# Six attention blocks ahead of the FFN instead of nine, ordered by a clock model, in a gated cross-attention and top-1 expert kernel

## The chip, the cores and the metric

The kernel runs on one core of a Trainium2 chip. The metric is the device time in microseconds (us) of one execution, as the median of several runs. A core has five engines that run side by side, each with its own queue of instructions: PE (TensorE, matrix products; its weight loads are shown as PEld), DVE (VectorE), ACT (ScalarE), POOL (GpSimd) and SP (SyncE, used here to issue transfers). ACT also issues some transfers from its queue. An engine takes its instructions strictly in the order in which the program lists them, and waits where one needs another engine's or a transfer's result.

## What is computed

For 4 batches of 2048 rows with 512 columns, all in float32:

```python
def _L0_xattn_ref(query, ref, Wq, bq, Wk, bk, Wv, bv):
    Q = query @ Wq + bq
    K = ref @ Wk + bk
    V = ref @ Wv + bv
    scores = jnp.einsum('bqh,bkh->bqk', Q, K)
    attn = jax.nn.softmax(scores, axis=-1) * norm_fact
    return jnp.einsum('bqk,bkh->bqh', attn, V)

def _L0_ffn_ref(x, Wr, br, W1, b1, W2, b2):
    scores = jnp.einsum('bh,he->be', x.mean(axis=1), Wr) + br
    top1 = jnp.argmax(scores, axis=-1)
    ...
    h = jax.nn.relu(jnp.einsum('bnh,bhf->bnf', x, w1) + c1[:, None, :])
    return jnp.einsum('bnf,bfh->bnh', h, w2) + c2[:, None, :]

x = x + jnp.tanh(g_xattn[0]) * _L0_xattn_ref(_layernorm(x), ctx_1024, ...)
x = x + jnp.tanh(g_ffn[0]) * _L0_ffn_ref(_layernorm(x), ...)
```

The context has 128 rows for each batch. There are 8 experts with W1 of 512 x 2048 and W2 of 2048 x 512; each batch uses one, chosen by the mean of its normalised rows, so the expert of a batch is known only when all of that batch's attention is done.

## The kernel before

**Attention** is cut into 16 blocks (4 batches of NBLK = 4 blocks of TB = 512 rows). The keys and the query matrix are folded into one matrix M for each batch (`keys`, L339; `values`, L370 makes V). A block (`attention`, L168) loads x (L179) and its transpose xT (L182); takes the row statistics on DVE (st, L189) with the inverse deviation rstd on POOL (L195); forms the scores psc = xT·M on PE (L204), which DVE scales into sc (L211); takes the maximum on DVE (nmax, L219) and the exponential on ACT (L222); transposes it on PE (pp, L231) with a copy pT by ACT (L234); multiplies by V on PE (pav, L245), with DVE adding the result into x (L249); takes statistics again; stores the new x to DRAM (x1d, L259); normalises it to z on ACT (L263), in place of x; transposes z on PE (pt, L278), with ACT copying to zT (L282) and adding up the columns (zsum); and stores zT to DRAM (z2d, L288). zT has a tile of its own in the pool of xT.

**The FFN** runs in 16 stages (batch, one of NF = 2 halves of its rows, one of two halves fh of the 2048 features). Each stage is `ffn1` (L748) and `ffn2` (L869). Both use a two-level scheme with 7 products in place of 8 at each level, so sums of weights and sums of z are needed as operands. X, Y and Q are the PSUM banks into which the products go (L631); ACT copies X to Y (L650) between products, and DVE, ACT and POOL build the results from them. The sums of z are made by `z_prepare` (L682: L706 outer on POOL or DVE, L702 inner on POOL) from z2d.

**Weights.** `stage_w1` (L536) and `stage_w2` (L553) load an expert's weights as `base` (L478, L487), make the sums on POOL (`outer_sums`, L445, four subtractions; `inner_sums` calls it on the inner level) and store the results to DRAM tensors W1d and W2d (L466). `fetch` (L590) brings the operands back into a ring of NW = 5 tiles w (L616), issued by SP in the order of their use. `route` (L398) finds the expert (pr, L409; ei, L423), reads the number into SP's register (L426) and loads b1T.

**Order around the change.** The program is written out by Python generators, and their interleaving is each engine's order; no scheduler changes it. Ahead of the FFN, EARLY = 9 blocks run as `streams`, each starting `skew` = 13 steps after the one before, and inside a block the tuple `lag` (AT_ONCE or, in the FFN, LATER) says how many steps to let pass at certain places. Every third step one piece of `others` (keys and values of batches 1 to 3) is put in. The end of batch 0's fourth block starts `first_expert` (L948): route, then `stage_first` (L493) on POOL, which sums the first half of W1 in four pieces; a store is issued AGE steps after its sum (`later`, `settle`). In the FFN, `tick` (L1028) is called between products and lets the remaining seven blocks (`slow`) and the staging of weights (`staged`) advance by counters with the rates PACE. Loads of x go by SP ahead of the FFN and by ACT in it.

Of the kernel before, what the change touches and what calls it, by code (L numbers as in the profile page):

```python
# [11 lines left out]
F32 = mybir.dt.float32  # L12
# [6 lines left out]
P = 128  # L19
# [70 lines left out]
def flamingo(tc, ctx, x, xT, cxT, g_x, g_f, WqT, Wk, Wv, bqk, bv, Wr, br, W1, b1, W2, b2, out):  # L90
# [43 lines left out]
    nc.vector.tensor_scalar(gx, gx, float(1.0 / np.sqrt(H).astype(np.float32)), None, ALU.mult)  # L134
    iota_e = const.tile([P, E], F32, name="iota_e")
# [8 lines left out]
    for b in range(B):  # L144
# [7 lines left out]
        for fh in range(2):  # L152
            for lo, n in ((0, 4), (4, 3)) if b + fh else ((0, 2), (2, 2), (4, 3)):
                t = dram.tile([P, n, 2, 7, P], F32, name=f"W1d_{b}{fh}{lo}")
                W1d.update({(b, fh, lo + i): (t, i) for i in range(n)})
            W2d[b, fh] = dram.tile([P, 2, 4, 2, Q], F32, name=f"W2d_{b}{fh}")

    zsum = {}
    MV = {}

# [5 lines left out]


    def attention(b, blk, pools):  # L168


        xp, xTp, wk, ps_t, ps_a, queue, lag = pools

        def wait(n):
            for _ in range(n):
                yield

        Mb, Vb = MV[b]
        xt = xp.tile([P, 4, H], F32, tag="x", name=f"x_{b}_{blk}")
        queue.dma_start(xt, rows(x, b, blk))  # L179
        yield from wait(lag[5])  # L180
        xTt = xTp.tile([P, KC, TB], F32, tag="xT", name=f"xT_{b}_{blk}")
        nc.sync.dma_start(xTt, xT[b, blk].rearrange("p c t q -> p c (t q)"))  # L182
        yield from wait(lag[6])

        def statistics():
            mv = small.tile([P, 4, 2], F32, tag="mv", name="mv", bufs=4)
            for t in range(4):
                st = small.tile([P, 6], F32, tag="st", name="st", bufs=4)
                nc.vector.bn_stats(st, xt[:, t, :])  # L189
                nc.vector.bn_aggr(mv[:, t, :], st)  # L190
                yield
# [4 lines left out]
            yield  # L196
            return mv, rstd

        _, rstd = yield from statistics()
        psc = ps_a.tile([P, 4, S], F32, tag="pa", name="psc")  # L200
        sc = wk.tile([P, 4, S], F32, tag="wk", name="sc")
        for t in range(4):
# [5 lines left out]
            if t % 2:  # L208
                yield
        for t in range(4):  # L210
# [4 lines left out]
            if t % 2:  # L215
                yield
# [3 lines left out]
        yield  # L220
        for t in range(4):
# [4 lines left out]
            if t % 2:  # L226
                yield
        yield from wait(lag[0])
# [3 lines left out]
        yield  # L232
        pT = wk.tile([P, TB], F32, tag="wk", name="pT")
        nc.scalar.copy(pT, pp)  # L234
        coef = small.tile([P, 4], F32, tag="coef", name="coef", bufs=4)
        nc.vector.reciprocal(coef, ssum)
        nc.vector.tensor_scalar(coef, coef, gx, None, ALU.mult)
        yield
        yield from wait(lag[1])
        pav = {}  # L240
        for t in range(5):
            if t < 4:
                ps, tag = ((ps_a, "pa"), (ps_t, "pt"))[t % 2]
                pav[t] = ps.tile([P, H], F32, tag=tag, name="pav")
                nc.tensor.matmul(  # L245
                    pav[t], lhsT=pT[:, t * P : (t + 1) * P], rhs=Vb, start=True, stop=True
                )
            if t:
                nc.vector.scalar_tensor_tensor(  # L249
                    xt[:, t - 1, :], pav[t - 1], coef[:, t - 1 : t], xt[:, t - 1, :],  # L250
                    ALU.mult, ALU.add,
                )
            yield
        mv, rstd = yield from statistics()
        yield from wait(lag[2])
        shift = small.tile([P, 4], F32, tag="shift", name="shift", bufs=4)
        nc.vector.scalar_tensor_tensor(shift, mv[:, :, 0], -1.0, rstd, ALU.mult, ALU.mult)
        yield
        queue.dma_start(x1d[b, blk], xt)  # L259
        yield from wait(lag[3])  # L260
        z = xt
        for t in range(4):
# [4 lines left out]
            yield  # L267
        yield from wait(lag[4])
        if blk == 0:
            zsum[b] = small.tile([P, KC, NBLK], F32, tag="zsum", name=f"zsum_{b}", bufs=2)  # L270
        zT = xTp.tile([P, KC, TB], F32, tag="xT", name=f"zT_{b}_{blk}")
        pt = {}
        for kc in range(KC + 1):
            if kc < KC:
                ps, tag = ((ps_t, "pt"), (ps_a, "pa"))[kc % 2]
                pt[kc] = ps.tile([P, TB], F32, tag=tag, name="pt")
                for t in range(4):
                    nc.tensor.transpose(  # L278
                        pt[kc][:, t * P : (t + 1) * P], z[:, t, kc * P : (kc + 1) * P], ident
                    )  # L280
            if kc:
                nc.scalar.activation(  # L282
                    zT[:, kc - 1, :], pt[kc - 1], AF.Copy,
                    accum_out=zsum[b][:, kc - 1, blk : blk + 1],
                )
            yield
        yield from wait(lag[7])
        queue.dma_start(z2d[b, blk], zT)  # L288
        yield
# [3 lines left out]
    xp, xTp, wkp = pool("xp", 1), pool("xTp", 1), pool("wk", 2)  # L293
    ps_t, ps_a = pool("ps_t", 1, space=PSUM), pool("ps_a", 1, space=PSUM)
    first, setup = ExitStack(), ExitStack()


    AT_ONCE, LATER = (4, 2, 3, 7, 4, 3, 8, 3), (2, 1, 3, 6, 3, 3, 8, 0)

    EARLY = 9  # L300
    three = (
        pool("x0", 5, first), pool("xT0", 3, first), pool("wk0", 4, first),
        pool("ps_t0", 2, first, space=PSUM), pool("ps_a0", 2, first, space=PSUM), nc.sync, AT_ONCE,
    )
    mv1 = pool("mv1", 1, first)
    one = (xp, xTp, wkp, ps_t, ps_a, nc.sync, AT_ONCE)
    ps_k = pool("ps_k", 2, first, space=PSUM)
    sp = pool("setup", 1, setup, side="right")
    if True:
        M0 = sp.tile([P, KC, S], F32, name="M0")  # L310
        V0 = sp.tile([P, H], F32, name="V0")
        MV[0] = (M0, V0)
        ctxT0 = sp.tile([P, 1, KC, S], F32, name="ctxT0")
        ctxTr = sp.tile([P, B - 1, KC, S], F32, name="ctxTr")
        w = {name: sp.tile([P, KC, H], F32, name=f"w{name}") for name in ("k", "q", "v")}
        nc.sync.dma_start(ctxT0, cxT[:, 0:1])
        for c in range(2):
            nc.sync.dma_start(w["k"][:, :, c * Q : (c + 1) * Q], Wk[:, :, c * Q : (c + 1) * Q])
        nc.sync.dma_start(w["q"], WqT)
        bvb = sp.tile([P, H], F32, name="bvb")  # L320
        with nc.allow_non_contiguous_dma(reason="bias"):
            nc.scalar.dma_start(bvb, bv.partition_broadcast(P))
        bqb = sp.tile([P, KC, P], F32, name="bqb")
        nc.vector.tensor_copy(bqb, bqk_t[:, 0:KC].unsqueeze(2).to_broadcast([P, KC, P]))
        order = [(b, blk) for b in range(B) for blk in range(NBLK)][:EARLY]
        streams = [attention(*i, one if i == order[-1] else three) for i in order]
# [3 lines left out]
        for m in range(KC):  # L330
            st = small.tile([P, 6], F32, tag="st", name="st", bufs=4)
            mq = small.tile([P, 2], F32, tag="mq", name="mq", bufs=2)
            nc.vector.bn_stats(st, w["q"][:, m, :])
            nc.vector.bn_aggr(mq, st)
            nc.vector.tensor_scalar(
                w["q"][:, m, :], w["q"][:, m, :], mq[:, 0:1], None, ALU.subtract
            )

        def keys(cT, n, KT, M, pc_out):  # L339

            for m in range(KC):
                pk = ps_k.tile([P, n, S], F32, tag="pk", name="pk")
                for kc in range(KC):
                    nc.tensor.matmul(  # L344
                        pk, lhsT=w["k"][:, kc, m * P : (m + 1) * P], rhs=cT[:, :, kc, :],
                        start=kc == 0, stop=kc == KC - 1,
                    )
# [4 lines left out]
                yield  # L352
            for kc in range(KC):
                pm = ps_k.tile([P, n, S], F32, tag="pk", name="pm")
                for m in range(KC):
                    nc.tensor.matmul(  # L356
                        pm, lhsT=w["q"][:, m, kc * P : (kc + 1) * P], rhs=KT[:, m, :],
                        start=m == 0, stop=m == KC - 1,
                    )
                nc.scalar.copy(M(kc), pm)  # L360
                yield
            pc = ps_k.tile([P, n * S], F32, tag="pk", name="pc")
            for m in range(KC):
                nc.tensor.matmul(
                    pc, lhsT=bqb[:, m, :], rhs=KT[:, m, :], start=m == 0, stop=m == KC - 1
                )
            nc.scalar.copy(pc_out, pc)
            yield

        def values(cT, V):  # L370
            pv = ps_k.tile([P, H], F32, tag="pk", name="pv")
            for kc in range(KC):
                nc.tensor.matmul(  # L373
                    pv, lhsT=cT[:, kc, :], rhs=w["v"][:, kc, :], start=kc == 0, stop=kc == KC - 1
                )
            nc.vector.tensor_tensor(V, pv, bvb, ALU.add)

# [342 lines left out]
    h = {}  # L720
# [374 lines left out]
```

## Time and profile before

| what | value |
|---|---|
| median of 3 runs | 1777.44 us (1776.56 to 1781.16) |
| profiled execution | 1777.29 us, of which the span of the core 1775.3 us |
| mean granted PE clock | 0.982 |
| busy: DVE, ACT, POOL | 1042.1, 581.2, 681.2 us |
| first FFN matmul | 193.76 us |
| z2d of the fourth block issued | 139.55 us |
| expert number ready; base load issued | 150.9; 153.06 us |

The span runs from the first to the last instruction of the profiled execution. Busy times are the sums of an engine's instructions; where an engine is not busy, it waits, and the profile names the instruction or transfer that ended the wait. The granted clock is the share of the full clock at which PE was allowed to run.

### The profile page before, as it was taken

The page shows a single profiled execution, that of the slowest core. Times are in us where ns is not written, and L with a number is a line of the kernel's source. Part 1 is how long each engine was busy: PE and PEld are TensorE (multiplying, and loading weights), DVE is VectorE, ACT ScalarE, POOL GpSimd, SP SyncE. Part 2 cuts the span into 40 slices and gives each one's busy share as a digit, 9 for nine tenths or more (in the row PEclk, how much of TensorE's full clock was granted, in tenths as well). Part 3 has the DMA queues.
Part 4 walks back from the last instruction along what each step waited for, and adds up shares of the span by engine and source line. Part 5 has one row for each costly group of instructions (what it writes and reads, how often), then busy time and mean ns, then how long its engine had stood idle before and what let it go on. Part 6 is the DMA issues. An engine that isn't in the chain of part 4 may idle for free.

```text
span 1775.3 us, 21897 instructions
## 1 busy us (share of the span) xinstructions
PE 1688.1 (95%) x7894; PEld 1432.4 (81%) x7894; DVE 1042.1 (59%) x1632; ACT 581.2 (33%) x1277; POOL 681.2 (38%) x564
## 2 busy tenths in 40 slices
PE   7977688999999899999999999999999999999998
PEld 5545477888878788888888888888888888888887
DVE  3678267584666647666564736474846463646362
ACT  1245531433415134251524323242424141415150
POOL 0128463476435454235532564056513410251010
PEclk9998899999999999999999999999999999999999
DMA  7487795786838678485856666565757452536241
GB/s 290 155 317 270 304 336 212 244 301 237 338 132 298 252 246 322 163 303 175 306 177 226 215 220 243 191 217 194 272 183 238 162 180 84 190 125 199 77 141 70
DMA packets 145562, 390.76 MB, mean 220 GB/s; under 512 B 10672, under 2 KB 40368, under 8 KB 130864
## 3 DMA queue, kind: packets, MB, share of 16 engines
q1 hardware_dynamic: 141568, 367.07, 58.6%
q10 hardware_dynamic: 3888, 22.31, 3.2%
q8 instruction: 63, 1.03, 0.2%
q14 instruction: 43, 0.35, 0.1%
HBM read 269.28 MB, written 120.06 MB: 219 GB/s over the span
## 4 chain that ended last, share of the span: by engine, by line
PE 86%; DVE 6%; DMA 4%; POOL 2%; issue 1%; ACT 0%; SPq 0%; DVEq 0%; POOLq 0%; ACTq 0%
PE Y L631 34%; PE Q L631 23%; PE X L631 22%; PE pav L245 2%; PE psc L204 2%; DVE st L189 1%; DMA w<-in_W_dram 1%; DVE h L726 1%; DVE y L894 1%; PE pt L278 1%; PE pk L344 1%; PE pm L356 1%; DMA W1d<-tt 1%; DVE x L249 1%; PE pv L373 1%; POOL tt L448 1%
## 5 line engine op out<-in xcount | busy, mean ns | idle before, releaser
L631 PE MATMUL Y<-z,w 128*128 128x256 f32 x1344 | 335.2, 383 | 15.1 <-DMA w<-W1d 5.8
L448 POOL TENSOR_TENSOR base<-base 128x512 f32<-128x512 f32 (+2 forms) x152 | 212.4, 1406 | 234.7 <-DMA base<-in_W_dram 207.1
L631 PEld LDWEIGHTS Y<-z,w 128*128 128x128 f32 x1344 | 252.2, 191 | 59.4 <-issue 9.8
L763 ACT ACTIVATE h<-c,b1T 128x256 f32<-128x256 f32 x512 | 229.9, 501 | 70.9 <-DVE c L791 29.6
L650 ACT COPY Y<-X 128x512 f32<-128x512 f32 x144 | 82.3, 571 | 469.4 <-PE X L631 469.2
L631 PE MATMUL X<-w,h 128*128 128x256 f32 x1024 | 230.0, 381 | 3.1 <-DMA w<-in_W_dram 3.0
L631 PE MATMUL Y<-w,h 128*128 128x256 f32 x1024 | 229.8, 382 | 0.0
L631 PE MATMUL Q<-w,h 128*128 128x256 f32 x1024 | 227.1, 379 | 0.0
L631 PEld LDWEIGHTS X<-w,h 128*128 128x128 f32 x1024 | 195.1, 191 | 34.2 <-issue 6.3
L631 PEld LDWEIGHTS Y<-w,h 128*128 128x128 f32 x1024 | 196.5, 192 | 30.7 <-issue 4.0
L631 PE MATMUL Q<-z,w 128*128 128x256 f32 x896 | 217.7, 383 | 0.6
L631 PE MATMUL X<-z,w 128*128 128x256 f32 x896 | 215.7, 380 | 1.6 <-DMA w<-W1d 1.6
L631 PEld LDWEIGHTS Q<-w,h 128*128 128x128 f32 x1024 | 194.2, 190 | 26.6 <-issue 0.5
L702 POOL TENSOR_TENSOR z<-z 128x256 f32<-128x256 f32 x224 | 185.9, 855 | 52.1 <-DMA z<-z2d 25.3
L631 PEld LDWEIGHTS Q<-z,w 128*128 128x128 f32 x896 | 171.0, 192 | 25.6 <-issue 1.2
L631 PEld LDWEIGHTS X<-z,w 128*128 128x128 f32 x896 | 170.0, 191 | 25.0 <-issue 2.0
L782 POOL TENSOR_TENSOR r<-r,cg 128x512 f32<-128x512 f32 x32 | 40.5, 1267 | 375.5 <-DVE cg L837 359.7
L195 POOL TENSOR_TENSOR rstd<-ve,mhalf 128x4 f32<-128x4 f32 x32 | 35.8, 1120 | 277.9 <-DVE ve L194 277.6
L631 PE MATMUL Y<-w,s 128*128 128x256 f32 x512 | 114.4, 379 | 0.0
L894 DVE SCALAR_TENSOR_TENSOR y<-Y,gf,y 128x512 f32<-128x512 f32 x64 | 47.9, 749 | 110.2 <-PE Y L631 109.2
L245 PE MATMUL pav<-V,pT 128*128 128x512 f32 x128 | 73.0, 681 | 37.9 <-DVE x L249 26.0
L631 PEld LDWEIGHTS Y<-w,s 128*128 128x128 f32 x512 | 96.7, 190 | 15.0 <-issue 2.4
(120 smaller groups left out, 1894.9 us busy)
## 6 DMA issues: line engine op xcount, KB each, us to landing
w<-W1d SPq DMA_DIRECT2D x112, 512.0 KB, 4.2
w<-W1d SPq DMA_DIRECT2D x112, 384.0 KB, 3.5
w<-W2d SPq DMA_DIRECT2D x64, 512.0 KB, 6.6
base<-in_W_dram SPq DMA_DIRECT2D x31, 1024.0 KB, 6.7
W1d<-base SPq DMA_DIRECT2D x14, 1792.0 KB, 10.9
w<-in_W_dram SPq DMA_DIRECT2D x48, 512.0 KB, 5.1
W1d<-tt SPq DMA_DIRECT2D x16, 1344.0 KB, 7.0
xT<-in_xT_dram SPq DMA_DIRECT2D x16, 1024.0 KB, 10.7
```

The lines of the kernel that those rows point to most:

```text
L189: nc.vector.bn_stats(st, xt[:, t, :])
L195: nc.gpsimd.tensor_tensor(rstd, ve, mhalf, ALU.pow)
L204: nc.tensor.matmul(psc[:, t, :], lhsT=xTt[:, kc, t * P : (t + 1) * P], rhs=Mb[:, kc, :], start=kc == 0, stop=kc == KC - 1,)
L245: nc.tensor.matmul(pav[t], lhsT=pT[:, t * P : (t + 1) * P], rhs=Vb, start=True, stop=True)
L249: nc.vector.scalar_tensor_tensor(xt[:, t - 1, :], pav[t - 1], coef[:, t - 1 : t], xt[:, t - 1, :], ALU.mult, ALU.add,)
L448: eng.tensor_tensor(o, l, r, ALU.subtract)
L631: nc.tensor.matmul(bank[:, c, :], lhsT=left(k, c), rhs=right(k, c), start=fresh and c == 0 and k == 0, stop=c == 1 and k == ks - 1, skip_g ...
L650: nc.scalar.copy(t["Y"], t["X"])
L702: nc.gpsimd.tensor_tensor(a[o], a[l], a[r], op)
L763: nc.scalar.activation(h[ij][:, v, 2 * m + c, :], src[:, c, :], AF.Relu, bias=b1T[:, f + c : f + c + 1],)
L782: eng.tensor_tensor(r[j], r[j], v, ALU.add)
L894: nc.vector.scalar_tensor_tensor(o, v, gf, o, ALU.mult, ALU.add)
```

## The change

1. EARLY is 6 instead of 9. The four blocks of batch 0 run at the same time; the fifth block follows the first, the sixth follows the fourth.
2. Each generator now yields which engine its piece uses and for how many us by an estimate in the source; a class `Stream` keeps a time for each stream, and the stream with the smallest time goes next. The counters `lag`, `skew`, `AGE`, `GAP` and `LOAD` are gone. `places` and `room` count the tiles of a pool that are in use, so that a stream asks before it takes one.
3. The keys are made for batch 0, batch 1, and batches 2 and 3 together, in three goes; M and V of batch 1 are copied by ACT (`second`) and not sent through DRAM.
4. The first half of W1 is summed as two streams (`first_half`: `part(0)` and `part(1)`); `minus` gives each subtraction to DVE or POOL, whichever the model has free earlier. Each result is stored as soon as it is there. The sums of z of the first FFN half are shared in the same way (`lefts_`).
5. z goes to the tile of xT, and zT to the tile of x, which has one buffer in the FFN. pT goes to sc's place.
6. In the FFN the two streams advance by the model's time and PACE.

The core of the diff:

```diff
-        yield from wait(lag[2])
         shift = small.tile([P, 4], F32, tag="shift", name="shift", bufs=4)
         nc.vector.scalar_tensor_tensor(shift, mv[:, :, 0], -1.0, rstd, ALU.mult, ALU.mult)
-        yield
+        yield (("DVE", 0.2),)
         queue.dma_start(x1d[b, blk], xt)
-        yield from wait(lag[3])
-        z = xt
+        z = xTt.rearrange("p c q -> p (c q)").rearrange("p (t h) -> p t h", t=4)
...
-        zT = xTp.tile([P, KC, TB], F32, tag="xT", name=f"zT_{b}_{blk}")
+        zT = xt.rearrange("p t h -> p (t h)").rearrange("p (c q) -> p c q", c=KC)
...
-    EARLY = 9
+    EARLY = 6
+    START, SLACK = (14.0, 1.0, 2.0, 3.0), 0.3
+    PRESS = 0.3
...
+    def second():
+        yield from until(lambda: 1 in ready_kv and all((0, i) in done_at for i in range(NBLK)))
+        Mb = mvp.tile([P, KC, S], F32, tag="M", name="M_1")
+        Vb = mvp.tile([P, H], F32, tag="V", name="V_1")
+        nc.scalar.copy(Mb, Ms[:, 0])
+        nc.scalar.copy(Vb, Vs[1])
+        MV[1] = [Mb, Vb]
+        yield (("ACT", 1.2),)
...
+    def minus(eng, o, l, r):
+        name = {nc.gpsimd: "POOL", nc.vector: "DVE"}.get(eng)
+        if name is None:
+            name = min(("DVE", "POOL"), key=lambda n: free[n])
+            eng = {"POOL": nc.gpsimd, "DVE": nc.vector}[name]
+        eng.tensor_tensor(o, l, r, ALU.subtract)
+        return ((name, 0.2 + 2.1e-3 * int(np.prod(o.shape[1:]))),)
...
-    def stage_first(eng, x0):
+    def first_half():
...
+        def outer(pc):
+            t4, t1, t2 = outs[pc]
+            b11, b21, b22, b12 = (blocks[pc][i // 2][:, i % 2] for i in range(4))
+            for i, took in enumerate(outer_sums(None, b11, b21, b22, b12, t4, t1, t2)):
+                yield took
+                if i == 1:
+                    for k in range(2):
+                        keep(5 + k, 1, pc, outs[pc][1 + k].unsqueeze(1))
+                if i == 2:
+                    keep(4, 1, pc, t4.unsqueeze(1))
+            keep(2, 2, pc, blocks[pc][1])
+        def part(pc):
+            yield (("DMA", 8),)
+            for i in range(2):
+                yield from inner_sums(None, blocks[pc][i])
+                if i == 0:
+                    keep(0, 2, pc, blocks[pc][0])
+            yield from outer(pc)
+            fetched[pc] = 1
...
+    class Stream:
+        def step(self):
+            if not ahead_of_ffn[0]:
+                self.at = max(self.at, clock["now"])
+            chains = next(self.gen, False)
...
+                    for engine, us in chain_:
+                        if not ahead_of_ffn[0]:
+                            t += us * BUSY[engine]
+                            if engine == "PE":
+                                clock["now"] += us
+                        elif engine in free:
+                            t = free[engine] = max(free[engine], t) + us
...
+    while True:
+        s_ = min(parts, key=lambda s: s.at)
...
+            if first_at is not None and clock["now"] >= first_at and fetched == [1, 1] and 1 in Zs[0, 0]["made"] and not any(
+                t in parts for t in threes
+            ):
+                break
+        if not s_.step():
+            parts.remove(s_)
...
-    PACE = {"slow": (0.6, 0.7, 0.7), "staged": (1.3, 0.7, 0.5, 0.5)}
+    PACE = {"slow": (1.0,.7,.7), "staged": (3.0,3.,3.,3.)}
...
+    def paced(name, stream, more):
+        due[name] = min(due[name] + more, 1.0 + more)
+        while stream and due[name] >= 1 and stream.at <= clock["now"] + SOON:
+            due[name] -= 1
+            if not stream.step():
+                stream = None
+        return stream
```

`keep` stores a result to W1d at once. The loop that writes the order ahead of the FFN ends when the first weights have been fetched, both parts of the first half are summed and the blocks of the three-buffer pools are written; what is left of the last block and of the first expert's staging goes into the FFN.

## The prediction

> **What bounds the kernel now.** I read the page first: the busy totals, the row of granted clock, the chain that ended last.
>
> ```profile
> PE 1688.1 (95%) x7894; PEld 1432.4 (81%) x7894; DVE 1042.1 (59%) x1632; ACT 581.2 (33%) x1277; POOL 681.2 (38%) x564
> ...
> PE   7977688999999899999999999999999999999998
> ...
> PE 86%; DVE 6%; DMA 4%; POOL 2%; issue 1%; ACT 0%; SPq 0%; DVEq 0%; POOLq 0%; ACTq 0%
> ```
>
> TensorE (PE) is the bound, with 86% of the chain; 1775.3 - 1688.1 = 87.2 us of its span are idle. The slices show where: the first seven, of 44.4 us each. So next I read the windows.
>
> ```profile
> 100.00:150.00 50.00, 36.55 (x195) 25.65 (x196) 40.21 (x102) 22.62 (x66) 26.50 (x27) 0.88 0.85 325
> 150.00:200.00 50.00, 29.10 (x132) 18.87 (x131) 26.79 (x62) 25.62 (x66) 39.58 (x40) 0.81 0.74 284
> 200.00:250.00 50.00, 41.45 (x183) 34.84 (x184) 21.24 (x37) 19.28 (x43) 19.39 (x16) 0.90 0.84 305
> ...
> 300.00:350.00 50.00, 48.66 (x220) 41.34 (x221) 24.08 (x39) 16.82 (x34) 15.47 (x13) 0.95 0.71 246
> ...
> 1000.00:1050.00 50.00, 50.00 (x233) 43.88 (x232) 24.73 (x27) 7.09 (x13) 38.59 (x37) 1.00 0.56 195
> ```
>
> After window and length come busy PE, PEld, DVE, ACT, POOL and the granted clock. An idle PE costs twice: 29.10 of 50 us busy in 150 to 200, and those at a clock of 0.81. By 1000 nothing is left to gain. The first FFN matmul stands at 193.76 in the timeline; 46.5 us of the idle time lie before it, 40.7 behind. The waits name them:
>
> ```profile
> PE pav L245 <- DVE x L249: 26.0, 10, 5.9
> PE pav L245 <- ACT pT L234: 11.9, 3, 6.9
> PE pt L278 <- ACT x L263: 9.2, 4, 8.5
> ...
> PE Y L631 <- DMA w<-W1d: 5.8, 1, 5.8
> PE Y L631 <- ACT Y L650: 4.6, 1, 4.6
> ```
>
> The columns are us in total, times, longest. Behind 193.76 the waits come to 34.5: pav 15.6 (seven blocks inside the FFN, 2.2 each), W1d 5.8 + 1.6, Y on ACT 4.6, and 6.9 for c, Q and weights. The four windows above that are not full cost a further (1 - clock) x busy; 200:250 gives 4.1 and 300:350 gives 2.4. For all of them behind 193.76 I take 14, what remains of the stretch when its matmuls at the full-clock rows' durations, the waits and a tail of 4.5 are taken off. So L, what the FFN part loses, is 34.5 + 14 = 48.5.
>
> What holds the FFN's start at 193.8 is the first expert's weight sums, which are serial on POOL (GpSimd):
>
> ```profile
> 163.69 5.33 POOL L448 TENSOR_TENSOR base<-base 128x256 f32<-128x256 f32 x7
> 169.13 1.02 POOL L195 TENSOR_TENSOR rstd<-ve,mhalf 128x4 f32<-128x4 f32 x1
> 170.12 6.67 POOL L448 TENSOR_TENSOR base<-base 128x256 f32<-128x256 f32 x9
> 176.74 2.10 POOL L448 TENSOR_TENSOR tt<-base 128x896 f32<-128x896 f32 x1
> 178.92 4.22 POOL L448 TENSOR_TENSOR tt<-base,tt 128x896 f32<-128x896 f32 x2
> ...
> 192.06 2.08 POOL L448 TENSOR_TENSOR tt<-base 128x896 f32<-128x896 f32 x1 [5.93 <-DMA W1d<-tt]
> ```
>
> They begin after routing: the base load is issued at 153.06, when the fourth block's z2d went out at 139.55.
>
> **The change, part by part.** Every step is a difference from span 1775.3; the profiled execution took 1777.3 (2.0 outside the span), beside a median of 1777.4.
>
> *Fewer blocks ahead.* A block costs PE 16 score matmuls of 0.2225 (3.57), four pp (0.45), four pav at full clock of 0.86 (3.45) and 16 transposes (1.75): 9.2 us. Three blocks go behind the FFN's start: 27.6, less 1.75, since the ninth's last transposes stood near it anyway: 26 us more behind the start. So the new span is 1775.3 + (T - 193.8) + 26.0 + (L' - 48.5), with T the first FFN matmul and L' the new loss. Break-even is T + L' = 216.3.
>
> *T.* Four blocks now run abreast. DVE bounds them: per block twice 4 x 0.85 + 0.17 statistics, 4 x 0.345 scores, 0.68, 0.37, 4 x 0.747 adds and 0.16, together 12.7; four make 51. With M_0 ready near 26 and V_0's add near 33, the last shift falls at about 79. Then z takes 4 x 0.81 on ACT; zT now overwrites x, so it waits for the x1d store (landing 10.6) issued at 79, and, with SP's load of block five ahead of that store, the fourth z2d goes out near 94. Routing took 139.55 to 150.9 before, in spaced steps; its instructions alone are about 5.5: 99.5. On SP the load of x for the sixth block stands ahead and waits for z2d to land (8.3), so the base load is issued at about 104, not 101. It lands in 6.5: 110.5.
>
> The sums are then split. In the built order POOL has of the first half 13 at 0.727, 4 at 2.2, five z sums (3.6) and two rstd (2.0): 24 us; DVE does the like beside it. Together they slow each other: POOL's 4.22 pair is 4.88 where DVE runs two-input sums, and I lengthen POOL by about a fifth: 140. Store 147 (6.3), and now what is queued behind it counts. POOL next has the second weight's base2 sums (load 6, four at 1.3, two z sums): 160. The rstd of the sixth block stands behind them, then its shift, z (3), 16 transposes (1.75) and the six opening matmuls (1.7), all ahead of the FFN on PE: T = 168. Behind base2's store on SP stand the first five weight loads, landing 167 to 170, which agrees. Bounds: 155 if base2's chain isn't waited for (140 + 6.3 + five loads at 4.2 partly abreast), 188 if the two streams lengthen each other as the longest row below (some 10 more) and SP's queue adds a landing of 10.
>
> *A rule against it.* The sums' conflict has a row of its own:
>
> ```profile
> L726 DVE TENSOR_TENSOR h<-h,h x64: 658/686/2562, 256.4 to 1724.4; 128x512 f32<-128x512 f32 x64
> ```
>
> Shortest, median and longest of one shape on DVE are 658, 686 and 2562 ns; two pairs beside POOL's sums, at 256.4 and 290.5, took 3.84 and 4.39 us against 1.3. The Trainium skill, "SBUF — State Buffer", section "Who interferes with whom", says that a DVE instruction with two SBUF inputs and a GpSimd one reading SBUF take a shared port pair as an exclusive lock, the second blocking until the first ends. By that rule two streams give nothing: DVE's overlapped sums would be added whole to POOL's, and T would be near 175. The row of 2562 speaks for it, the POOL pair of 4.88 for less; the sum above goes by the pair, and the rule's case lies within the bounds.
>
> *L'.* The stores of W1d have landed before T, so the first waits (5.8, 1.6, 4.6) go. The start itself keeps 4.5 for the first Y copy and the slow clock (0.63 to 0.85 in the windows of 180 to 210). Pav: ten blocks; where they lie in ffn2, as before, 2.2 each, four blocks; in ffn1, where PE has 2 to 3 us of other products between two pav, 0.3 each, six blocks: 10.6. Other waits keep 6.2.
>
> New is the swap: zT lies in x's tile, so the next block's x load, which follows directly on ACT's queue, waits until z2d has landed (6.7 median in the FFN). Before, x's tile had been free since z. Behind it on ACT stand Y<-X and the relus, and PE waits for Y within one product (eight matmuls of 0.216, 1.7 us, in ffn1; 3.5 in ffn2). Bounds: nothing if always covered; 50 if seven of ten blocks stop PE for 5.4 and the clock falls with it. Four holds lie in ffn1 and would cost 6.7 - 1.7 - a further product or so: 2.5 each, so 10. Idle so far 31; the clock takes 0.27 us for each of them (before: 14 for 34.5 is 0.41, though a part of it belongs to the start): 8.4. L' = 39.7, bounds 15 (no pav, no x waits) to 80.
>
> Edits taken at nothing: M_1 and V_1 copied by ACT (1.2, while PE still has blocks; if uncovered, 1.2 once); pT in sc's place (an order it had anyway); the sums for later stages, hidden by 18 us or more of margin behind PE's products (if late, one landing of 10).
>
> Sum: 1775.3 - 25.8 + 26.0 - 8.8 = 1766.7; with 2.0 outside it, 1769.
>
> **The rivals.** *ACT's queue becomes the bound (slower).* For it: the x load stands directly behind the z2d store, and 6.7 exceeds both slacks. Against: ffn2's relu-free stretches hide a part. Price: seven holds of 5.4 less 10 counted, 28, with 0.36 of clock 38: span 1805; with half of it 1786, device 1788 to 1807. It decides from 3 or 4 full holds that stop PE (216.3 - 207.7 = 8.6, /1.36 = 6.3 more idle, which gives break-even). I give 0.27.
>
> *The start is held (about even).* POOL's and SP's queues keep T at 183, the first conflict and base2 in full: 1784 by the sum; with T at 178, 1779. For it: rstd stands behind base2's sums. Against: those sums are few. 0.19.
>
> *The front gives all it can.* T = 158, ffn1's pav and the swap cost nothing: L' near 28: span 1775.3 - 35.8 + 26 - 20.5 = 1745, device 1747. For it: ACT is busy 16.82 of 50 at 300, so it has room. Against: 6.7 is fixed. 0.20.
>
> *The clock model orders otherwise than it means to:* the order of built instructions shows six blocks and two streams, so I leave it no chance of its own.
>
> **How the numbers follow.** Likeliest, as summed, 0.34: 1769, of its own 1757 to 1780. What a measurement can tell is 0.3%, 1772.1 to 1782.8. Faster: 0.25 of the likeliest, all 0.20 of the last rival, 0.04 of the held start, 0.02 of ACT's: 0.51. Same: 0.08 + 0.08 + 0.03 = 0.19. Slower: 0.01 + 0.07 + 0.22 = 0.30. The range 1744 to 1797 leaves out one tenth at each end.
>
> **What would show it.** The timeline gives T (155 to 188) and the base load near 104. PE's busy time stays within 15 of 1688, for its work is the same and only the clock moves it. Waits: W1d and ACT Y at the start gone; pav L245's wait under 15 behind the start; a new wait of Y or Q on ACT or on DVE x of 5 to 15. If PE's waits on ACT's queue exceed 25, the slower rival holds; if T is over 180, the second. I am wrong altogether if more than a few us are lost behind 600, in the staging of later experts.

## The result, and the profile after

| | median | lowest to highest | runs |
|---|---|---|---|
| before | 1778.65 us | 1775.51 to 1783.44 | 20 |
| changed | 1782.59 us | 1778.43 to 1794.17 | 20 |

The ratio is 1.0027, with a 95% interval of 1.0013 to 1.0041: the changed kernel is slower by a little, where 1769 had been forecast. The profiled execution took 1780.24 us with a span of 1778.5. In these 20 runs each the changed kernel spreads over 15.7 us, the one before over 7.9; in the later sessions the kernel before itself spread over 10.3 to 12.7. The granted clock goes with the time: 0.983 in the changed kernel's run of 1778.43, 0.977 in that of 1794.17.

In the page of the changed kernel, the busy time of PE and the two rows of slices (tenths of 40 equal parts of the span):

```profile
PE 1691.3 (95%) x7966; PEld 1442.8 (81%) x7966; DVE 1025.5 (58%) x1656; ACT 581.9 (33%) x1284; POOL 650.2 (37%) x543
...
PE   6876899998998999999999999999999999999998
...
PEclk8988999999999999999999999999999999999999
```

PE is busy for 1691.3 us (1688.1 before); idle are again 87.2. The hole is shallower (the fourth to seventh slice, 133 to 311 us, were 7, 6, 8, 8 before and are 6, 8, 9, 9), but the first two slices, with 6 and 8 in place of 7 and 9, are emptier. The windows of the same kernel (length, busy PE, PEld, DVE, ACT, POOL, clock, DMA share, GB/s):

```profile
100.00:150.00 50.00, 36.06 (x174) 27.21 (x173) 42.56 (x68) 11.02 (x35) 36.88 (x32) 0.90 0.66 259
150.00:200.00 50.00, 37.01 (x133) 25.82 (x132) 16.92 (x36) 15.84 (x32) 15.71 (x16) 0.83 0.92 329
200.00:250.00 50.00, 46.44 (x212) 38.11 (x211) 33.58 (x61) 19.53 (x45) 23.10 (x16) 0.97 0.69 241
400.00:450.00 50.00, 43.74 (x192) 36.95 (x191) 23.97 (x42) 24.49 (x51) 29.71 (x24) 0.93 0.95 337
```

From 150 to 250 PE is busy for 83.45 us where it was 70.55, and 200 to 250 has a clock of 0.97 in place of 0.90. That is the gain. It is given back: 26 us of attention now lie behind the FFN's start, and new losses appear there, such as the window from 400 to 450 with 43.74 at 0.93. The same window of the kernel before:

```profile
400.00:450.00 50.00, 48.25 (x227) 40.96 (x226) 23.23 (x38) 16.65 (x35) 28.73 (x28) 1.00 0.72 254
```

Next come the first FFN matmul in PE's timeline of the changed kernel (start, length), and PE's longest waits behind it (total, times, longest):

```profile
175.72 1.03 PE L727 MATMUL X<-z,w 128*128 128x256 f32 x4
```

```profile
PE Y L727 <- DMA w<-W1d: 9.5, 5, 3.3
PE Y L727 <- DVE Q L927: 6.0, 5, 2.8
PE pav L281 <- ACT sc L258: 2.4, 3, 1.1
PE pav L281 <- DVE x L269: 2.2, 1, 2.2
```

T is 175.72. By the prediction's own identity, L' = 1778.5 - (1775.3 - 18.1 + 26.0 - 48.5) = 43.8: of these 31.1 are waits and 12.7 the rest. Part of the rest is the clock: (1 - clock) x busy PE, added up over windows of 50 us behind T, gives 8.1 (14.0 before). What makes up the other 4.6 wasn't found. The front gained 18.1 us and the FFN part lost 4.7 us less than before, together 22.8, against 26.0 us of work moved. That is the whole result: 3.2 us longer.

Why T is 175.7 and not 168 can be read in the queues. In the timeline of the changed kernel (start, length, engine, line), SP's instructions:

```profile
107.04 0.33 SPq L198 DMA_DIRECT2D x<-in_x_dram  x1
...
109.62 0.36 SPq L509 DMA_DIRECT2D b1T<-in_b_dram  x1
110.16 0.61 SPq L557 DMA_DIRECT2D base<-in_W_dram  x1
...
164.25 0.32 SPq L549 DMA_DIRECT2D W2d<-base  x1
...
167.39 7.39 SPq L710 DMA_DIRECT2D w<-W1d  x5
```

The base load goes out at 110.16, not at 104. Two things hold it. The load of the sixth block's x (107.04) stands ahead and waits for the fourth block's z2d to land. And the expert's number comes late, as the timeline shows, with POOL's sums of z beside two of DVE's instructions:

```profile
103.52 4.65 POOL L531 TENSOR_TENSOR z<-z,z 128x1024 f32<-128x1024 f32 x2 [12.80 <-DVE rsc L493]
...
103.75 2.15 DVE L498 TENSOR_SCALAR key<-rsc,top 128x8 f32<-128x8 f32 x1
105.93 2.26 DVE L499 TENSOR_TENSOR key<-key,iota_e 128x8 f32<-128x8 f32 x1
```

The two on DVE work on 8 elements per partition, yet take over 2 us each; POOL runs two 128x1024 sums of z, of 2.34 us each, from 103.52 to 108.17. Then the sums take 29.0 us from 117.85 to 146.83 (29.5 forecast). Behind them POOL has base2's sums, and behind those the rstd of the sixth block:

```profile
157.82 1.26 POOL L531 TENSOR_TENSOR base<-base 128x512 f32<-128x512 f32 x1 [5.18 <-DMA base<-in_W_dram]
...
162.96 1.26 POOL L531 TENSOR_TENSOR base<-base 128x512 f32<-128x512 f32 x1
164.18 1.01 POOL L213 TENSOR_TENSOR rstd<-ve,mhalf 128x4 f32<-128x4 f32 x1
```

The DVE addition that makes V of batch 3 stands behind that block's shift (165.22), and SP's store of that V (166.04) ahead of the weight loads (167.39). This is the chain that the prediction named, 4 us later than it said. A last wait of ACT makes up the rest:

```profile
170.67 0.60 ACT L308 ACTIVATE x<-pt 128x512 f32<-128x512 f32 x1 [2.33 <-DMA x1d<-x]
```

zT overwrites x, and so the copy must wait until the store of x1d has landed.

### The profile page after: what moved, and what is told of

Its sections match the earlier page's. It is cut to its first block, busy times and chain, and to the rows that moved or that the text cites. A ratio compares the mean times of both kernels' runs of the same rounds, so it can differ in the third digit from the quotient of the medians.

```text
span 1778.5 us, 22053 instructions
## 1 busy us (share of the span) xinstructions
PE 1691.3 (95%) x7966; PEld 1442.8 (81%) x7966; DVE 1025.5 (58%) x1656; ACT 581.9 (33%) x1284; POOL 650.2 (37%) x543
## 4 chain that ended last, share of the span: by engine, by line
PE 48%; DMA 1%; DVE 1%; issue 0%; ACT 0%; DVEq 0%
PE Y L727 20%; PE Q L727 13%; PE X L727 13%; DMA w<-W1d 1%; PE psc L227 0%; PE pav L281 0%; PE pt L321 0%; DVE c L896 0%; DVE cg L944 0%; DVE Q L927 0%; ACT h L868 0%; DVE c L940 0%; DVE s L922 0%; PE pp L255 0%; DVE y L1001 0%
## 5 line engine op out<-in xcount | busy, mean ns | idle before, releaser
L531 POOL TENSOR_TENSOR base<-base 128x512 f32<-128x512 f32 (+1 forms) x142 | 198.0, 1402 | 211.7 <-DMA base<-in_W_dram 201.4
L727 PEld LDWEIGHTS X<-z,w 128*128 128x128 f32 x896 | 170.6, 192 | 26.9 <-issue 3.7
L531 POOL TENSOR_TENSOR z<-z 128x256 f32<-128x256 f32 x163 | 138.2, 871 | 54.9 <-DVE z L531 37.8
L1001 DVE SCALAR_TENSOR_TENSOR y<-X,gf,y 128x512 f32<-128x512 f32 x32 | 23.9, 746 | 133.2 <-issue 94.7
```

Source lines behind the costliest of these rows:

```text
L531: eng.tensor_tensor(o, l, r, ALU.subtract)
L727: nc.tensor.matmul(bank[:, c, :], lhsT=left(k, c), rhs=right(k, c), start=fresh and c == 0 and k == 0, stop=c == 1 and k == ks - 1, skip_g ...
L1001: nc.vector.scalar_tensor_tensor(o, v, gf, o, ALU.mult, ALU.add)
```

## The experiments

Each kernel was timed beside the kernel before on the same chip; the ratios are against that one. T is the first FFN matmul of the run's profile, L' what the FFN part loses, worked out from that profile's span as above.

| run | what is edited | median, us | ratio (95%) | T | L' |
|---|---|---|---|---|---|
| changed kernel | | 1782.59 | 1.0027 (1.0013 to 1.0041) | 175.7 | 43.8 |
| e1 | z sums behind routing | 1779.12 | 1.0000 (0.9979 to 1.0021) | 170.6 | 42.9 |
| e2 | base2 begun in the FFN | 1824.53 | 1.0241 (1.0218 to 1.0263) | 167.7 | 97.5 |
| e3 | no swap of tiles in the FFN | 1804.44 | 1.0132 (1.0108 to 1.0157) | 176.6 | 67.6 |
| e4 | shared sums on DVE alone | 1829.99 | 1.0278 (1.0256 to 1.0301) | 176.0 | 96.3 |
| e5 | e1, sixth x loaded by ACT | 1780.16 | 0.9986 (0.9965 to 1.0006) | 170.2 | 49.7 |
| e6 | EARLY = 5 | 1840.56 | 1.0332 (1.0304 to 1.0360) | 153.2 | 116.7 |
| e7 | staging placed sooner | 1866.78 | 1.0476 (1.0448 to 1.0504) | 181.0 | 122.5 |
| e8 | shared sums on POOL alone | 1824.94 | 1.0237 (1.0209 to 1.0265) | 173.0 | 93.5 |
| e9 | e5, rstd ahead of base2 | 1778.16 | 0.9983 (0.9966 to 1.0001) | 171.3 | 42.4 |
| e10 | kernel before, EARLY = 8 | 1803.82 | 1.0124 (1.0098 to 1.0150) | 192.8 | 65.8 |
| e11 | e2, short waits in staging | 1777.28 | 0.9971 (0.9953 to 0.9988) | 168.4 | 51.7 |
| e12 | e5 and e11 | 1775.91 | 0.9967 (0.9948 to 0.9987) | 166.1 | 47.7 |

For e6 the moved work is 35.2 and not 26.0, for e10 it is 7.4. T and L' come from a single profile each. The profiles of e1, e9 and the changed kernel took 4.9, 3.7 and 2.4 us less than their medians, that of e11 3.6 more, so their L' are low or high by about as much; for the time, the ratios are the better guide.

### What holds the start of the FFN: e1, e5, e9

```diff
 # e1
         z = yield from z_load(0, 0)
+        yield from until(lambda: 0 in expert)
         yield from z_outer(z, None)
 # e5, on top
-        queue.dma_start(xt, rows(x, b, blk))
+        (nc.scalar if (b, blk) == order[-1] else queue).dma_start(xt, rows(x, b, blk))
# e9, on top: in attention, behind the second statistics
+        done_at["rstd", b, blk] = 1
# and in stage_w2, behind the first load of base2
+            if (b, fh, kp) == (0, 0, 0):
+                yield from until(lambda: ("rstd", *order[-1]) in done_at)
```

> Edit: the sums of z of the first FFN half are listed behind the routing of batch 0, not ahead of it. Nothing is left out. In the trace of the changed kernel the two small DVE operations of routing (128x8) took 2.15 and 2.26 us while POOL ran a 128x1024 sum of z (4.65 us for two), and one DVE sum of z waited 2.33 us for its load ahead of them. Theory A (the front's chain runs through routing): these two shrink to some 0.2 us, the base load is issued near 105 instead of 110.2, and the first FFN matmul T comes 4 to 5 us earlier than 175.7, the time falls by 3 to 5 us. Rival B (what comes after the FFN's start decides, the front's end is held elsewhere): the base load is earlier, T moves by less than 2 us, the time is the same within 2 us. Rival C (the sums moved behind routing now stand between the weight sums): T later by 2 to 4 us.

> Edit: as e1 (sums of z behind routing), and the sixth block's x is loaded by ACT's queue, not SP's. Nothing is left out. With e1 the expert's number was ready at 104.85, yet the base load went out only at 109.63, as in the changed kernel (110.16): on SP the sixth block's load of x stood ahead and waited until z2d of the fourth block had landed. Theory A2 (that load, a consequence of zT in x's tile, holds the base load): base load at 105 to 106, the last first-half sum 3 to 5 us earlier than 146.8, the first FFN matmul T 2 to 4 us earlier than e1's 170.6, and the time 3 us or more under e1's 1779. Rival B2 (POOL's sums and the sixth block are bound by other work): base load earlier, T within 1.5 us of 170.6, the time within 2 us of e1's.

> Edit: as e5, and on POOL the rstd of the sixth block's second statistics is listed ahead of the base2 sums; the load of base2 stays where it was (near 151). Nothing is left out. Theory A (the sixth block's chain through rstd, DVE's shift and V, SP's store of V and the weight loads holds T): in e5 rstd came 4 to 5 us after it was ready; it comes at once, the weight loads go out near 157 to 159, T at 164 to 167 (170.2 in e5), and as staging isn't moved the time falls by 2 to 5 us against e5's 1780. Rival (T is paid back by weights that are no earlier): T falls, the waits for W1d and W2d behind T grow by as much, the time is within 2 us of e5's.

In e1 the same two DVE instructions, with no POOL sum beside them:

```profile
104.04 0.23 DVE L498 TENSOR_SCALAR key<-rsc,top 128x8 f32<-128x8 f32 x1
104.31 0.17 DVE L499 TENSOR_TENSOR key<-key,iota_e 128x8 f32<-128x8 f32 x1
```

They take 0.23 and 0.17 us, and the expert's number is there at 104.85. But the base load goes out at 109.63, only 0.5 earlier: theory A had the conflict right and its place wrong, since SP's load of x holds the base load anyway. T still fell by 5.1. The order on POOL and DVE had moved too: the shift of the sixth block came at 160.14 (165.22), and the weight loads at 162.73, now ahead of the store of W2d. In e5 the base load does come earlier, at 107.10, and the store of the first half's last sums at 143.86 (146.74 in e1); but base2's load still went out at 150.94 (151.52), and T fell by 0.5 alone. Base2 loads into the tile from which those last sums are stored, and that store took 7.1 us to land in place of 4.8. So A2 holds for the base load and fails for T: the 2.9 us that the sums gained did not reach the load behind them. In e9 the rstd comes as soon as its input is there (154.46), the weight loads at 160.37, and still T is 171.3. The timeline shows what took over:

```profile
166.20 0.60 ACT L309 ACTIVATE x<-pt 128x512 f32<-128x512 f32 x1 [7.41 <-DMA x1d<-x]
...
166.94 1.97 PE L322 MATMUL pt<-ident,xT 128*128 128x128 f32 x8 [6.80 <-ACT x L309]
```

ACT waits 7.41 us for the store of x1d to land before it may write zT into x's tile; PE's remaining transposes, which stand ahead of the FFN in its queue, wait 6.80 for ACT. The swap's own wait is next in line as soon as the rest comes earlier. Against e5 the time is the same within the intervals. No run kept the sixth block alone from waiting for that store, so how far T would fall without it isn't shown.

### Why later weights can't wait: e2, e4, e8, e7, e11

```diff
 # e2: in first_expert
         bias2_load(0)
+        yield from until(lambda: not ahead_of_ffn[0])
         yield from stage_w2(0, 0, nc.gpsimd)
 # e4, e8: in minus
-            name = min(("DVE", "POOL"), key=lambda n: free[n])
+            name = "DVE"
 # in e8
+            name = "POOL"
 # e7: in stage_w1 and stage_w2
-            yield (("DMA", 9),)
+            yield (("DMA", 6),)
...
-            yield (("DMA", 10),)
+            yield (("DMA", 5),)
 # e11: e2, and in the same places
+            yield (("DMA", 5 if b == 0 else 9),)
...
+            yield (("DMA", 3 if b == 0 else 10),)
```

> Edit: the second weight's sums (base2) of the first expert are begun only once the FFN has begun. Nothing is left out. Theory A: in the changed kernel POOL's base2 sums (157.8 to 164.2) stand ahead of the sixth block's rstd, DVE's shift and V of batch 3 behind it, SP's store of that V, and the first weight loads at 167.4; with them out of the way rstd comes near 159, the weight loads near 161, T at 167 to 170, and the time falls by 5 to 8 us, if ffn2's weights are still in time. Rival B (the FFN's start is not what decides): T falls as said, but the time by less than 2 us, since a new wait for W2d of 4 us or more appears behind T. Rival C: W1d's stores hold the weight loads at 167 anyway, T stays within 2 us of 175.7.

> Edit: the subtractions that were given to whichever of DVE and POOL is free earlier all go to DVE (the first half's weight sums and the first sums of z). Nothing is left out. Alone, one 128x256 sum is 0.41 us on DVE and 0.73 on POOL, one of 128x896 is 1.08 against 2.07. Theory A (two streams on DVE and POOL slow each other, and gain little): 32 x 0.41 + 8 x 1.08 = 22 us of DVE's time for the weights beside POOL's 29 in the changed kernel, and DVE has some 14 us of attention and 8 us of z sums beside them: the last first-half sum ends at 140 to 150 (146.8 before), T within 4 us of 175.7, routing's small operations back to 0.2 us and T 4 us earlier at best. Rival (two streams do share the work): the sums end 10 us or more later, near 157 to 160, T and the time rise by 8 us or more.

> Edit: the subtractions that were given to whichever of DVE and POOL is free earlier all go to POOL. Nothing is left out. POOL takes over 32 - 13 = 19 or so sums less those of z: in the changed kernel DVE did 3 + 1 of 128x256 and 4 of 128x896 for the weights and 5 + 1 for z. Theory A (two streams gain something): 4 x 0.73 + 4 x 2.07 + 5 x 0.73 + 2.35 = 17 us more on POOL, less what the two lose to each other (the shared sums took 2.93 to 2.99 for 2.07 and 0.9 to 1.0 for 0.73, some 5 us): the last first-half sum ends some 10 us later than 146.8, the second weight's first load with it, and by e2's and e4's proportion the time rises by 20 to 35 us. Rival (by the exclusive port DVE's share is lost to POOL anyway): the sums end within 4 us of 146.8, the time within 8 us.

> Edit: in the clock model, the time that the staging of later weights lets pass for a load goes from 9 to 6 us and for a store from 10 to 5; its instructions are the same and stand earlier in the queues. Nothing is left out. Runs e2 and e4 had the second weight's first load 14.5 and 15.8 us later (165.9 and 167.2 against 151.4) and were 42 and 47 us slower, with PE waiting 24 and 15 us for one W1d operand: so staging has no slack. Theory D (the changed kernel already loses PE time to late weights, 9.5 + 1.2 us of waits for W1d behind T, and the clock with it): those waits fall under 4 us and the time by 5 to 12 us. Rival (placed earlier, POOL's sums wait for their loads at the head of its queue and hold the sums r and u that PE's chain needs): the W1d waits fall, waits of Y and Q on DVE and ACT grow by as much, the time is the same or higher.

> Edit: as e2 (the sums of base2 begin once the FFN has begun), and in the clock model the staging of the first expert lets pass 5 us for a load and 3 for a store, not 9 and 10; later experts as before. Nothing is left out. In e2 T was 167.7, 8 us earlier, but PE then waited 24 us for a W1d operand near 270, 8.3 for W2d and 12.6 for W2 operands. By the source's own waits and sums (1.1 x (9 + 10) + 5 us for each of two loads of W2, 1.1 x (9 + 10) + 13 for each of two of W1) staging takes 120 us if begun in the FFN, longer than one stage of some 105 us; with the short waits it takes 72. Theory E (these waits in the source's order, not an engine, made e2's 45 us): the wait of 24 is under 3, T stays at 167 to 169, the time falls by 30 us or more against e2's 1824.5, to 1770 to 1785. Rival (POOL or the transfers themselves are too slow): the 24 falls by less than half, time over 1805.

e2 gave T = 167.7, within its expectation: base2's sums, rstd, V and the weight loads were the chain. That it equals the prediction's 168 is chance. 168 was the sum with base2 in the chain; without it the prediction had 155. In e2 rstd starts at 156.86, as soon as its input is there, and the first weight loads go out at 159.64, so the sixth block's own end sets T. But by the ratios the kernel became 2.1%, 38 us, slower than the changed one. From the waits of PE behind T in e2:

```profile
PE X L727 <- DMA w<-W1d: 24.0, 1, 24.0
...
PE X L727 <- DMA w<-in_W_dram: 12.6, 1, 12.6
```

The wait ends at 300.57: one operand of the next stage came 24 us late. e4 and e8 say the same from another side. Sharing the sums does pay: the last one ends at 146.8 in the changed kernel, at 155.8 on POOL alone, at 161.6 on DVE alone, where sums stand between attention's instructions. So e8's theory A had the sums right, and in e4 the rival had. But T hardly moved (176.0, 173.0), and the time rose by more than any of them said, by 2.5% and 2.1%, 45 and 37 us. It rose behind T again, with X waiting 15.1 and 16.3 us for W1d until 310.0 and 300.6. In all three base2's first load had moved from 151.4 to 161.5, 165.9 or 167.2.

The kernel before began that load at 205.4, 11.6 us behind its T, and waited 3.0 us in all for later weights. The difference is in the source: the changed kernel lets 9 us pass for every load and 10 for every store of the staging, times 1.1 in the FFN, one after the other. e11 shortens these for the first expert and leaves e2's late start as it is. The longest wait for W1d on X becomes

```profile
PE X L727 <- DMA w<-W1d: 4.1, 1, 4.1
```

(24.0 in e2), T is 168.4, and the median falls by 47 us, the ratio to 0.9971. So neither POOL nor the transfers were too slow; the order written from the model's waits was. That e4 and e8 lost their time in the same way is argued from the later load and the wait for W1d; neither was run with the short waits. e7 shortened them for all experts and began them ahead of the FFN, and went the other way. T came at 181.0: SP had the second load of base2 (170.23) ahead of the first weight loads (172.98). Behind T, in PE's waits of e7:

```profile
PE Y L727 <- DMA w<-W1d: 51.7, 11, 10.1
PE X L727 <- DMA w<-W1d: 17.9, 3, 13.3
```

Y alone waited 51.7 us for W1d (of X's 17.9, 1.1 stand just ahead of T). Neither theory foresaw that; in both these waits were to fall. Whether SP's order or the transfers' share made them grow was not separated.

### How many blocks ahead: e6, e10

```diff
 # e6
-    EARLY = 6
+    EARLY = 5
 # e10, the kernel before
-    EARLY = 9
+    EARLY = 8
```

> Edit: five attention blocks ahead of the FFN, not six. Nothing is left out. 9.2 us of PE's work goes from ahead of the FFN to behind its start. Theory A (a block ahead costs the start less than the 9 us that it saves behind, since PE is idle 50 us there): T comes 0 to 6 us earlier than 175.7 and the time rises by 3 to 9 us. Rival (the last block ahead holds the start by as much as it saves): T falls by 9 us or more, the time is the same or lower.

> Edit: the kernel before with eight blocks ahead of the FFN, not nine; nothing else. Nothing is left out. 9.2 us of PE's work less 1.75 goes behind the FFN's start, or 7.4. Theory A (there T is set by routing and POOL's sums, not by the ninth block): T within 4 us of 193.8, the time up by 4 to 9 us. Rival (a block taken from the front gives back its whole length, and the blocks behind are hidden in waits of PE's): T falls by 7 us or more and the time by 0 to 3 us. As e6, where five blocks in place of six cost 58 us with T 22.5 us earlier, hints: if the time rises by over 20 us, the FFN part's hand-placed order doesn't bear one more block.

With five blocks T is 153.2, 22.5 us earlier for 9.2 us of work moved. By the identity alone this should win 13 us; it lost some 55 (3.3% against 0.3%). From PE's waits behind T in e6:

```profile
PE Y L727 <- DMA w<-W1d: 20.6, 4, 8.9
PE X L727 <- DMA w<-W1d: 17.6, 3, 9.4
PE X L727 <- DMA w<-in_W_dram: 15.8, 4, 7.1
```

These sum to 54.0, but 7.6 of X's 17.6 are the wait that ends at T itself. Behind T late weights cost some 46 us, against 10.7 in the changed kernel. In the kernel before, one block fewer moved T by 0.9 us and added 22.7 us to the median for 7.4 us of work; its waits for W1d behind T went from 7.4 us to the following in e10:

```profile
PE Y L631 <- DMA w<-W1d: 18.6, 9, 4.8
PE X L631 <- DMA w<-W1d: 16.6, 4, 5.7
```

They sum to 35.2. So neither version's FFN part bears a further block at the price of its matmuls. That the order which interleaves blocks, staging and products is fitted to the number of blocks is a reading that agrees with both runs; no run tested it. The expectations of 3 to 9 and 4 to 9 us were both far off. More than six blocks ahead were not tried in the changed kernel.

### The swap of tiles: e3, and the best version: e12

```diff
 # e3: in attention
-        z = xTt.rearrange("p c q -> p (c q)").rearrange("p (t h) -> p t h", t=4)
+        swap = ahead_of_ffn[0]
+        z = xTt.rearrange("p c q -> p (c q)").rearrange("p (t h) -> p t h", t=4) if swap else xt
...
-        zT = xt.rearrange("p t h -> p (t h)").rearrange("p (c q) -> p c q", c=KC)
+        if swap:
+            zT = xt.rearrange("p t h -> p (t h)").rearrange("p (c q) -> p c q", c=KC)
+        else:
+            zT = xTp.tile([P, KC, TB], F32, tag="xT", name=f"zT_{b}_{blk}")
```

> Edit: blocks inside the FFN put z back into x's tile and zT into a tile of its own in xT's pool, as the kernel before did; ahead of the FFN nothing changes. Nothing is left out. Theory A (the hold of ACT's queue until z2d has landed is mostly hidden): PE's waits on ACT behind T (4 to 7 us) and the time fall by 0 to 3 us, and xT's load, which now waits for z2d, shows on SP. Rival (the hold is the loss of the FFN part): the time falls by 8 us or more, and the waits of Y on DVE and ACT (some 12 us) go.

> Edit: e11's two edits on top of e5 (sums of z behind routing, sixth x loaded by ACT). Nothing is left out. Theory E with A: T at 163 to 167, no wait over 5 us for W1d near 270, the time 3 to 8 us under the changed kernel's. Rival as for e11: over 1805.

Without the swap the kernel is 1% slower than with it; neither theory had that sign. It isn't a pure undo: the step counts that had hidden the store of x1d are gone, and z in x's tile must wait for that store. The waits of ACT in e3 show it (48.5 us in eight blocks):

```profile
ACT x L297 <- DMA x1d<-x: 48.5, 8, 8.6
```

PE's waits behind T sum to 47.8 us there, 31.1 with the swap; that the wait for x1d is what lengthened them is argued, not shown. So the swap pays in this order. What it costs was seen in the changed kernel: between the store of z2d and the next load of x lie 4.8 to 10.5 us in each of ten blocks, 86 us in all. In half of them ACT still does some work in between; directly ahead of the load it stands idle for 1.4 to 8.8 us, 62 in all. PE's waits for ACT behind T sum to 9.1 us. Some more reach PE through DVE: at 186 ACT had stood 5.5 us ahead of its copy s, most of it for a load of x; DVE waited 5.1 for that copy, and PE 2.8 for DVE (its longest wait for Q).

e12 puts the good edits together. T is 166.1, within what was expected, and X's wait for W1d in the second stage is 3.1 us. The first FFN matmul in the timeline of PE in e12:

```profile
166.09 1.77 PE L727 MATMUL X<-z,w 128*128 128x256 f32 x4
```

Its ratio is 0.9967 (0.9948 to 0.9987): it beats the kernel before by 5 us of median on the same chip (1781.16), and the changed kernel, by the two ratios, by some 0.6%. The waits for W1d between 400 and 450, 6.3 us in the changed kernel, are 7.4 here; that the transfers are the cause (a DMA share of 0.95 in that window) is argued and not shown.

## Why the prediction was wrong, point by point

- **T.** Forecast 168, measured 175.7; this is the step that failed, worth 7.7 of the 11.8 us by which the span exceeds the sum of 1766.7. The chain was the right one in the changed kernel, since taking base2 out of it brings T forward by 8.0 (e2), where the prediction's bound of 155 made it 13. But three terms were short: the base load went out 6.2 later than 104, since the fourth z2d left at 97 and not 94 and took 10 to land ahead of SP's load of x, with routing's small DVE instructions as late for another reason; its landing took 7.7, not 6.5; and the wait for the x1d store under zT (2.33 on ACT), which was counted for the fourth block, was left out for the sixth. Added up: the sums ended 6.8 later than 140; base2's load stood only 4.6 behind them where about 7 had been counted, so rstd came 4.2 later than 160; and from there to T it took 11.5 and not 8. The runs bear the step out. In e12 T is 166.1, and of the 0.74% between the forecast (0.9953 of the time before) and the changed kernel 0.60% are gone; e1, e5, e9 and e11, with T earlier by 4.4 to 7.3, are 0.27 to 0.56% faster than the changed kernel, each uncertain by some 0.2%. (e11 and e12 also place the staging anew.)
- **The sums.** The two streams took 29.0 us against 29.5. Lengthening POOL by a fifth was right as a sum, and e4 and e8 show that sharing saves 9 and 15 us of the end of the sums over one engine. By the rule of the port the prediction had T near 175, and T came there for other reasons. Its sentence that two streams give nothing by that rule does not follow: one sum of 128x896 takes 1.08 on DVE and 2.07 on POOL, so a share given to DVE shortens the whole even if the two never overlap.
- **L'.** 39.7 forecast, 43.8 measured. The waits alone were 31.1 against 31 by a cancelling of errors: pav 4.6 and not 10.6, the waits for W1d 10.7 where none was forecast. The rest was 12.7 and not 8.4. The windows put 8.1 of it down to the clock, near the 8.4 that the prediction had for it; so, as far as a clock of two digits tells, the 4.1 by which L' was short lie in the 4.6 that have no name yet.
- **Edits taken at nothing.** The margin of 18 us or more for later weights wasn't there. This sentence of the prediction is the one the runs contradict most. In the changed kernel itself it shows only as 10.7 us of waits for W1d; but a first load of base2 that is 10 to 16 us later costs 37 to 45 us (e2, e4, e8), until the source's waits are shortened (shown for e2's by e11).
- **The price of a moved block.** The prediction charged 26 us of plain PE time for three blocks. With six that held within the 4 us of L'. e6 and e10 show that it isn't a price one may extrapolate.
- **The rivals.** ACT's queue as the bound is refuted in the changed kernel: it stands idle for 62 us ahead of the ten loads of x, and PE's waits for ACT are 9.1 in all, 11.9 with the one that came through DVE. Even all its waits that aren't for a weight, 20.4, stay under the 25 that the prediction had named as the sign. The held start comes nearest: for T of 178 it had 1779, and the profile has 175.7 and 1780.2. Its chance had been put at 0.19.
- The profiled execution was 2.35 us under its median, that of before 1.36; so about 1 us of the miss isn't in the profile at all.

## What to carry to other kernels

Moving work behind the start of a stage that binds PE pays only if the start comes earlier by more than that work. Read what ends last at the start in each queue, not only on the engine that does the most: here it was a load on SP that waited for a tile, a tiny rstd behind sums, and a store under a reused tile, one after the other as each was removed. When an order is written from a model's estimates, those estimates are waits: check that a chain of them fits into the stage that has to hide it, and test a lateness of 10 us before calling it margin.

## What the runs showed of the hardware

A DVE instruction can be held for the whole of a POOL instruction however small it is: 128x8 operations took 2.15 and 2.26 us beside POOL sums of 2.34, and 0.23 and 0.17 alone (e1); a 128x4 shift took 2.02 us beside a 128x896 sum and 0.16 alone. POOL suffers too: its 128x896 sums took 2.93 to 2.99 us beside DVE's, and 2.07 alone. They took turns: the one of 2.99 began at 141.64, just behind a DVE sum of the same size (141.61, 1.07), and 1.07 + 2.07 is 3.14. The Trainium skill, "SBUF — State Buffer", section "Who interferes with whom", has this lock for DVE instructions with two SBUF inputs against GpSimd reads, and the whole wait agrees with it. The one of 2.15 has a single tile and an operand per partition; by that section it would contend only in a two-port mode, and no run shows whether it ran in one. The rule speaks of a full block, and the rows at 141.6 agree with it. Two streams still ended 9 us sooner than POOL alone, where each of these sums takes twice as long as on DVE, and 15 us sooner than DVE alone, whose sums stand between attention's instructions.

A short stop of PE can halve its clock for a while. In the changed kernel waits of 2.82, 2.95 and 3.31 us (ending at 189.13, 414.39 and 438.64) are each followed by some 3 us at a granted clock of 0.50; in e12 a wait of 3.10 (ending at 282.12) is followed by 1.00.

The changed kernel's 20 runs had granted clocks of 0.976 to 0.983. What makes the clock differ between runs of one program was not found.
